# A selective scan laid out as 8 channels by 16 states on the partitions

## The chip, the cores and the metric

The kernel runs on one core of a Trainium2 chip. The time is device time in microseconds (us), from one launch; the figure compared is the median of runs. The engines are TensorE (PE), VectorE (DVE), ScalarE (ACT) and GpSimd (POOL); SyncE (SP) issues nearly all DMAs.

## What is computed

Two "metaformer" layers on x of 2 x 96 channels x 128 x 128 pixels, fp32. Layer 0's mixer is four selective scans (Mamba) over the 16,384 pixels in four orders: by rows, by rows backwards, by columns, by columns backwards. Cut to the part that matters (192 inner channels, 16 states, rank 6):

```python
xc, z = split(x @ in_w.T);  xc = silu(causal_conv4(xc) + conv_b)
dt_raw, B, C = split(xc @ xproj_w.T)             # 6, 16, 16
dt = softplus(dt_raw @ dt_w.T + dt_b);  A = -exp(A_log)
h_t[d, s] = exp(dt_t[d] * A[d, s]) * h_{t-1}[d, s] + dt_t[d] * u_t[d] * B_t[s]
y_t[d]    = sum_s h_t[d, s] * C_t[s]             # u is xc
out = ((y + Dp * xc) * silu(z)) @ outp_w.T       # four of these, then a fusing matmul
```

Before it stands a channel layernorm; after it a quantised FFN, a 3 x 3 convolution and a second FFN.

## The kernel before

For each of the 2 batches three stages run: `normalize`, `mamba`, `ffn_and_conv`. Only `mamba` is touched by the change.

`mamba` runs the four directions as two pairs (by rows with by columns; the two backward ones). A pair has 2 x 192 = 384 channels, three groups `g` of 128. A **step** is 512 tokens of one pair: 2 pairs x 32 = 64 steps a batch. Within a step there are 24 **units**; a unit is one group and two states. The tokens lie along the free dimension, 128 channels on the partitions. Group 1 holds 64 channels of each direction, interleaved by small DMAs (`mix`).

For a unit the work is:
- SP fetches, by DMA from DRAM, the rows of B and of C for four states, spread over the 128 partitions (`row_tile`, line 335; 1 MB each, one of each for two units).
- POOL makes dt x u x B for four states (`b_part`, line 339), and adds what the state entering the step brings to the first token (343).
- ACT makes `da` = exp(dt x A), two states, into PSUM (`decay`, 349); `da` has three buffers of two PSUM banks.
- DVE runs the recurrence over 512 tokens as one scan instruction for each state (`scan`, 353).
- DVE multiplies by C (line 441); for one unit in four (`BY_POOL`) POOL does it (360).
- ACT copies the last token's state to `hst` (442).
- PE adds the states up in PSUM, with an identity as weights (`sums`, 357), onto y, which starts as Dp x xc (448). At a group's end DVE multiplies y by silu(z) (`gated`, 364), and PE projects (372, 374).

The order of instructions on every engine is written out by hand. One loop over all units k issues, in this order: the fetch for unit k+6 and POOL's product for unit k+2 (both for even k), slot (k, 0), the first scan of unit k, what stands `behind` unit k-1 (its product with C, the `hst` copy, the sums), `decay` for unit k+2, the second scan of unit k, the fetch of C, slot (k, 1). The slots hold the next step's prologue (input DMAs, convolution and gate matmuls and their evictions by ACT, silu, the rows of dt, B and C, softplus, dt x u), placed by a list of unit numbers (lines 308 to 323). All prologue matmuls and the projection share one PSUM bank, `misc`. Each engine takes its instructions strictly in this order. Silu and softplus each load another activation table, and exp's table is loaded again after them (`preload_act_table_set`).

Of the kernel before, what the change touches and what calls it, by code (L numbers as in the profile page):

```python
# [23 lines left out]
T = 512  # L24
# [9 lines left out]
C_AHEAD = 2  # L34
AHEAD = 2
BY_POOL = tuple((g, s) for g in range(3) for s in (0, 8))
# [5 lines left out]
def tile_metaformer(ctx: ExitStack, tc: tile.TileContext, a: dict, out: bass.AP):  # L42
# [38 lines left out]
    amat = cpool.tile([128, 2, NG, S], F32, name="amat")  # L81
# [3 lines left out]
    def prep(st):  # L85
# [9 lines left out]
        alog, dskip = load("alog", (128, 2, NG, S)), load("dskip", (128, 2, NG))  # L95
# [89 lines left out]
    def mamba(acc, xnr, xnc):  # L185

        with ExitStack() as st:
            pool = lambda n, bufs, **kw: st.enter_context(tc.tile_pool(name=n, bufs=bufs, **kw))

            io, gen, one, mixp, two = (pool(*p) for p in (("io", 2), ("gen", 4), ("one", 1), ("mixp", 1), ("two", 2)))  # L190
# [3 lines left out]
            hst = one.tile([128, NG, S], F32, name="hst")  # L194
            enter = one.tile([128, NG, S], F32, name="enter")
# [5 lines left out]
            def inproj(pi, g, w, src, taps):  # L201

                ps = misc()
                for k in taps:
                    se = {"start": k == taps[0], "stop": k == taps[-1]}
                    for d, rows, lo, hi in (
                        ((0, slice(0, 128), 0, 128),),
                        ((0, slice(0, 64), 128, 192), (1, slice(64, 128), 0, 64)),
                        ((1, slice(0, 128), 64, 192),),
                    )[g]:  # L210
                        nc.tensor.matmul(ps[rows, :], w(PAIRS[pi][d], k, lo, hi), src[d][:, k : k + T], **se)  # L211
                return ps

            def prologue(pi, i, d):
# [5 lines left out]
                def load():  # L220
# [9 lines left out]
                    d["dtu"], d["yg"] = [], []  # L230

                def conv(g):
                    d["ps"] = inproj(pi, g, lambda dd, k, lo, hi: inx[:, dd, k, lo:hi], src, (0, 1, 2, 3))

                def conv_out(g):
                    if g == 1:
                        d["xc"] = two.tile([128, NG, T], F32, name="xc")
                    t = mixed("xc") if g == 1 else d["xc"][:, g, :]
                    nc.scalar.activation(t, d["ps"], AF.Identity, bias=convb[:, pi, g : g + 1])  # L239

                def gate(g):
                    d["ps"] = inproj(pi, g, lambda dd, k, lo, hi: inz[:, dd, lo:hi], src, (3,))

                def gate_out(g):
                    if g == 1:
                        d["sz"] = two.tile([128, NG, T], F32, name="sz")
                    nc.scalar.copy(mixed("sz") if g == 1 else d["sz"][:, g, :], d["ps"])  # L247

                def mixed(name):
                    d["mix", name] = mixp.tile([128, T], F32, name="mix")  # L250
                    return d["mix", name]

                def mix(name):

                    for k in range(2):
                        nc.sync.dma_start(d[name][k:128:2, 1, :], d["mix", name][64 * k : 64 * k + 64, :])
# [17 lines left out]
                def rows_to_dram():  # L274

                    d["bcd"] = rows_d.tile([2, S // 4, 2, 4, T], F32, name="bcd")
                    nc.sync.dma_start(d["bcd"].rearrange("k q d s t -> (k q d s) t"), d["rows"][BCO:, :])


# [11 lines left out]
                def softplus(lo, hi):  # L291
                    t = d["dt"][:, lo:hi, :]
                    nc.scalar.activation(t, t, AF.Softplus)
                    nc.scalar.preload_act_table_set("natural_log_exp_and_others")

                def dt_u(g):
                    dtu = gen.tile([128, T], F32, name="dtu")
                    nc.gpsimd.tensor_tensor(dtu, d["dt"][:, g, :], d["xc"][:, g, :], ALU.mult)  # L298
                    d["dtu"].append(dtu)

                def entry(g):

                    nc.scalar.activation(enter[:, g, :], amat[:, pi, g, :], AF.Exp, scale=d["dt"][:, g, 0:1])

                first = pi == 0 and i == 0
                at = [(-3, 1, load), (3, 0, partial(mix, "xc")), (11, 0, partial(silu, "xc"))]
                at += [(9, 0, partial(mix, "sz")), (31, 1, partial(silu, "sz"))]
                at += [(12, 0, rows), (13, 1, rows_out), (14, 0, rows_to_dram)]  # L310
                for g, k in ((1, 1), (0, 5), (2, 9)):
                    at += [(k, 0, partial(conv, g)), (k + 1, 1, partial(conv_out, g))]
                for g, k in ((1, 7), (0, 18), (2, 21)):
                    at += [(k, 0, partial(gate, g)), (k + 1, 0, partial(gate_out, g))]
                soft = ((0, 1, 16), (1, 3, 26)) if first else ((0, 3, 17),)
                for x0, x1, k in soft:
                    at += [(k, 1, partial(softplus, x0, x1))]
                for g, k in enumerate((14, 24, 25) if first else (14, 15, 16)):
                    at += [(k, 0, partial(dt_in, g)), (k + 1, 0, partial(dt_out, g))]
                for g, k in enumerate((19, 27, 29)):  # L320
                    at += [(k, 0, partial(dt_u, g))]
                    if i > 0:
                        at += [((20, 24, 29)[g], 1, partial(entry, g))]
# [5 lines left out]
            def row_tile(d, g, s, k, ahead):  # L329

                t = gen.tile([128, 4, T], F32, name=f"row{k}", bufs=ahead + 1)

                src = d["bcd"][k, s // 4] if g == 1 else d["bcd"][k, s // 4, g // 2 : g // 2 + 1]
                n = src.shape[0]
                nc.sync.dma_start(t, src[None].broadcast_to((128 // n, n, 4, T)))
                return t

            def b_part(i, d, g, s, b):
                nc.gpsimd.tensor_tensor(b, d["dtu"][g][:, None, :].broadcast_to((128, 4, T)), b, ALU.mult)  # L339
                if i > 0:  # L340
                    if s == 0:
                        nc.gpsimd.tensor_tensor(enter[:, g, :], enter[:, g, :], hst[:, g, :], ALU.mult)
                    nc.gpsimd.tensor_tensor(b[:, :, 0], b[:, :, 0], enter[:, g, s : s + 4], ALU.add)

            def decay(pi, d, g, s):

                da = ps_w.tile([128, 2, T], F32, name="da")
                for j in range(2):
                    nc.scalar.activation(da[:, j, :], d["dt"][:, g, :], AF.Exp, scale=amat[:, pi, g, s + j : s + j + 1])  # L349
                return da  # L350

            def scan(j, da, b, h):
                nc.vector.tensor_tensor_scan(h[:, j, :], da[:, j, :], b[:, j, :], 0.0, ALU.mult, ALU.add)  # L353

            def sums(s, y, c):
                for j in range(2):
                    nc.tensor.matmul(y, ident, c[:, j, :], start=False, stop=s + j == S - 1)  # L357

            def by_pool(h, c):
                nc.gpsimd.tensor_tensor(c, h, c, ALU.mult)  # L360

            def gated(pi, d, g, y):
                t = d["sz"][:, g, :]
                nc.vector.tensor_tensor(t, y, t, ALU.mult)  # L364
                d["yg"].append(t[:, ::-1] if pi == 1 else t)
# [18 lines left out]
            units = [(g, s) for g in range(NG) for s in range(0, S, 2)]  # L384
# [30 lines left out]
            def fetch(k, n, ahead, m):  # L415
                if k < total:
                    t = row_tile(state[k // nu], *units[k % nu], n, ahead)
                    m[k], m[k + 1] = t[:, 0:2, :], t[:, 2:4, :]
                    if n == 0:
                        quads[k] = t  # L420

            def feed(k):

                if k < total:
                    n = k // nu
                    b_part(steps[n][1], state[n], *units[k % nu], quads.pop(k))

            def feed_decay(k):
                if k < total:
                    n = k // nu  # L430
                    das[k] = decay(steps[n][0], state[n], *units[k % nu])
# [3 lines left out]
            def behind(k):  # L435

                n, u = divmod(k, nu)
                (pi, i), d, (g, s) = steps[n], state[n], units[u]
                h, c = hs.pop(k), cs.pop(k)
                if (g, s) not in BY_POOL:  # L440
                    nc.vector.tensor_tensor(c, h, c, ALU.mult)  # L441
                nc.scalar.copy(hst[:, g, s : s + 2], h[:, :, T - 1])  # L442
                if s == 0:
# [8 lines left out]
                if (g, s) in BY_POOL:  # L452
                    later(k + 1, 1, True, by_pool, h, c)
                    later(k + 3, 1, True, sums, s, y, c)
                else:
                    sums(s, y, c)
                if k == total - 1:
                    gated(pi, d, g, y)
                if s == S - 2 and g > 0:
                    later(k + 4, 0, True, project, pi, i, d, g)  # L460
                    later(k + 5, 1, False, collect, pi, d, g)

            for m, (n, ahead) in ((bs, (0, B_AHEAD)), (cs, (1, C_AHEAD))):
                for k in range(ahead):
                    fetch(2 * k, n, ahead, m)
# [3 lines left out]
            for k in range(total + 6):  # L469
                n, u = divmod(k, nu)  # L470
                if u == nu - 3:

                    prepare(n + 2)
                if k % 2 == 0:
                    fetch(k + 2 * B_AHEAD, 0, B_AHEAD, bs)
                    feed(k + AHEAD)
                issue(k, 0)
                if k < total:
                    (g, s) = units[u]
                    da, b = das.pop(k), bs.pop(k)  # L480
                    hs[k] = b if (g, s) in BY_POOL else da
                    scan(0, da, b, hs[k])
# [3 lines left out]
                if k < total:  # L486
                    scan(1, da, b, hs[k])
                if k % 2 == 0:
                    fetch(k + 2 * C_AHEAD, 1, C_AHEAD, cs)
# [110 lines left out]
def _layout(v):  # L600
# [4 lines left out]
    perm = np.arange(2 * DI)  # L605
# [63 lines left out]
```

## Time and profile before

| | us |
|---|---|
| median of 3 runs | 11,546.39 (11,545.31 to 11,548.33) |
| the profiled execution | 11,556.77 |
| its span, first to last instruction | 11,555.0 |
| PE busy | 10,435.0 |
| DVE busy | 10,421.6 |
| POOL busy | 9,672.3 |
| ACT busy | 7,901.7 |

Busy time is the union of an engine's instructions over the whole span. A matmul's record overlaps the next one's, so PE's busy share says less than the distance between starts. A group line gives line, engine, operation, output <- inputs, shapes and count; then busy us and the mean ns of one; then the engine's idle time just ahead of these instructions and what ended most of it. A time line gives start, duration, engine, line and tile names. An fp32 matmul appears as two records.

### The profile page before, as it was taken

How to read it: one execution, taken by the hardware profiler on the slowest of the kernel's cores; microseconds unless marked ns; L12 is line 12 of the kernel's file. 1: busy time of each engine (PE TensorE's matmuls, PEld its weight loads, DVE VectorE, ACT ScalarE, POOL GpSimd, SP SyncE). 2: the span in 40 equal slices, each digit the busy share in tenths (PEclk: the TensorE clock that was granted, in tenths of full speed). 3: DMA queues.
4: the chain of work that ended last, by engine and by line, in shares of the span. 5: the costliest groups of instructions: out<-in, count | busy, mean ns of one | idle time of the engine just before them, and what ended most of it. 6: DMA issues, size and time to landing. Idle time of an engine off the chain costs nothing. (4 is left out here: it accounts for less than half of the span.)

```text
span 11555.0 us, 94102 instructions
## 1 busy us (share of the span) xinstructions
PE 10435.0 (90%) x24208; PEld 3971.4 (34%) x24208; DVE 10421.6 (90%) x10127; ACT 7901.7 (68%) x13564; POOL 9672.3 (84%) x4700
## 2 busy tenths in 40 slices
PE   7999999999999999989989999999999999999899
PEld 2333333333333333333323333333333333333333
DVE  6999999999999999994469999999999999999944
ACT  6767767677677677665567677677676776776655
POOL 5999999999999999991159999999999999999911
PEclk8999999999999999999989999999999999999999
DMA  7888888888888888880068888888888888888800
GB/s 263 335 329 333 333 332 332 330 331 333 329 332 333 330 331 333 329 322 19 26 243 334 328 331 334 330 333 333 333 331 329 332 332 329 331 333 329 319 13 13
DMA packets 540755, 3416.96 MB, mean 296 GB/s; under 512 B 67532, under 2 KB 68652, under 8 KB 143832
## 3 DMA queue, kind: packets, MB, share of 16 engines
q1 hardware_dynamic: 539960, 3410.16, 76.8%
q8 instruction: 196, 3.21, 0.1%
q14 instruction: 343, 2.81, 0.1%
q0 software_dynamic: 256, 0.79, 0.0%
HBM read 3289.04 MB, written 54.53 MB: 289 GB/s over the span
## 5 line engine op out<-in xcount | busy, mean ns | idle before, releaser
L339 POOL TENSOR_TENSOR row<-dtu,row 128x2048 f32<-128x2048 f32 x1536 | 6948.9, 4524 | 283.3 <-DMA row<-bcd 281.6
L357 PE MATMUL y<-row,ident 128*128 128x512 f32 x12288 | 5690.6, 603 | 700.0 <-DVE row L441 699.9
L353 DVE TENSOR_TENSOR_SCAN da<-da,row 128x512 f32<-128x512 f32 x4608 | 5456.9, 1214 | 38.9 <-ACT da L349 5.2
L349 ACT ACTIVATE da<-dt,amat 128x512 f32<-128x512 f32 x6144 | 4246.9, 691 | 170.2
L357 PEld LDWEIGHTS y<-row,ident 128*128 128x128 f32 x12288 | 2256.8, 190 | 4008.4 <-issue 2243.5
L441 DVE TENSOR_TENSOR row<-da,row 128x1024 f32<-128x1024 f32 x2304 | 2776.7, 1205 | 70.2 <-DMA row<-bcd 70.0
L442 ACT COPY hst<-da 128x2 f32<-128x2 f32 x2304 | 368.9, 160 | 2652.2 <-DVE row L441 2649.3
L360 POOL TENSOR_TENSOR row<-row,row 128x1024 f32<-128x1024 f32 x768 | 1807.4, 2353 | 223.0 <-DVE row L353 147.5
L353 DVE TENSOR_TENSOR_SCAN row<-da,row 128x512 f32<-128x512 f32 x1536 | 1852.4, 1206 | 91.9 <-POOL row L339 84.1
L211 PE MATMUL misc<-xa,inx 96*64 96x512 f32 (+1 forms) x2048 | 946.1, 605 | 50.0 <-ACT mix L239 26.8
L211 PE MATMUL misc<-xb,inx 96*64 96x512 f32 (+1 forms) x2048 | 952.3, 608 | 33.6 <-ACT hst L442 24.2
L564 POOL TENSOR_TENSOR acc<-acc,y 96x512 f32<-96x512 f32 x128 | 147.4, 1151 | 991.5 <-DVE y L563 991.5
L298 POOL TENSOR_TENSOR dtu<-dt,xc 128x512 f32<-128x512 f32 x384 | 487.4, 1269 | 106.0 <-DMA xb<-xnc 99.8
L576 PE MATMUL pc<-pad,kw 96*96 96x512 f32 x1152 | 566.4, 593 | 0.0
L211 PEld LDWEIGHTS misc<-xa,inx 96*64 96x64 f32 (+1 forms) x2048 | 327.3, 165 | 581.2 <-issue 438.0
L448 PE MATMUL y<-xc,dmat 128*128 128x512 f32 x768 | 419.5, 628 | 103.6 <-DVE sz L364 103.6
L374 PE MATMUL misc<-sz,gmat 128*96 128x512 f32 x1024 | 484.1, 595 | 0.0
L284 PE MATMUL misc<-rows,dtw 12*128 12x512 f32 x768 | 434.3, 645 | 50.6 <-ACT dt L289 37.9
L364 DVE TENSOR_TENSOR sz<-y,sz 128x512 f32<-128x512 f32 x384 | 264.6, 689 | 229.5 <-PE y L357 198.0
L136 DVE TENSOR_TENSOR xq<-xm,rs 96x512 fp8e5<-96x512 f32 x128 | 87.9, 687 | 392.2 <-ACT rs L132 392.2
L211 PEld LDWEIGHTS misc<-xb,inx 96*64 96x64 f32 (+1 forms) x2048 | 316.5, 164 | 361.9 <-issue 214.1
L372 PE MATMUL misc<-acc,ident 96*96 96x512 f32 x512 | 387.6, 842 | 57.3 <-ACT sz L247 53.8
(76 smaller groups left out, 7449.9 us busy)
## 6 DMA issues: line engine op xcount, KB each, us to landing
row<-bcd SPq DMA_DIRECT2D x3072, 1024.0 KB, 7.4
xc<-mix SPq DMA_DIRECT2D x256, 128.0 KB, 5.4
sz<-mix SPq DMA_DIRECT2D x256, 128.0 KB, 8.9
xa<-xnr SPq DMA_DIRECT2D x124, 193.1 KB, 8.6
xb<-xnc SPq DMA_DIRECT2D x124, 193.1 KB, 8.7
bcd<-rows SPq DMA_DIRECT2D x128, 128.0 KB, 9.5
acc<-in_x_dram SPq DMA_DIRECT2D x16, 768.0 KB, 5.7
xnr<-xn SPq DMA_DIRECT2D x16, 768.0 KB, 4.3
```

The costliest lines, as they stand in the source:

```text
L211: nc.tensor.matmul(ps[rows, :], w(PAIRS[pi][d], k, lo, hi), src[d][:, k : k + T], **se)
L284: nc.tensor.matmul(d["ps"], w, d["rows"][0 : 2 * RK, :], start=True, stop=True)
L298: nc.gpsimd.tensor_tensor(dtu, d["dt"][:, g, :], d["xc"][:, g, :], ALU.mult)
L339: nc.gpsimd.tensor_tensor(b, d["dtu"][g][:, None, :].broadcast_to((128, 4, T)), b, ALU.mult)
L349: nc.scalar.activation(da[:, j, :], d["dt"][:, g, :], AF.Exp, scale=amat[:, pi, g, s + j : s + j + 1])
L353: nc.vector.tensor_tensor_scan(h[:, j, :], da[:, j, :], b[:, j, :], 0.0, ALU.mult, ALU.add)
L357: nc.tensor.matmul(y, ident, c[:, j, :], start=False, stop=s + j == S - 1)
L360: nc.gpsimd.tensor_tensor(c, h, c, ALU.mult)
L374: nc.tensor.matmul(d["po"], gmat[:, pi, 2 * g - 2 + k, :], d["yg"][g - 1 + k], start=False, stop=k == 1)
L441: nc.vector.tensor_tensor(c, h, c, ALU.mult)
L448: nc.tensor.matmul(y, dmat[:, pi, g, :], d["xc"][:, g, :], start=True, stop=False)
L576: nc.tensor.matmul(pc, kw[:, t, :], rows, start=t == 0, stop=t == 8)
```

## The change

The partitions of a scan now hold 16 states x 8 channels, states outermost (p = 8 s + c), in place of 128 channels of one state.

- B and C depend on the state and the token alone, so one spread tile for a step and both directions (`bc`, 1 MB) replaces the fetched rows. It is written to DRAM and read back once a step (`rows_to_dram`, `spread`).
- dt x u depends on the channel, so it has to be spread over the 16 states: it is written to DRAM by four DMAs for each group, and `quad_tile` reads 4 x 8 channels back, spread over the states, 1 MB for two units. POOL multiplies it by B in place (`b_part`).
- dt is spread by PE: two matmuls a unit with a 0/1 matrix `sel`, each over 32 rows of the array, into the `da` banks; ACT takes exp in place.
- The entering state: two ACT products on the first token of `da`, and a scan that starts from 1, replace POOL's additions.
- The sum over states is a matmul with a 0/1 matrix `fold` whose output is 32 partitions wide: four for two units, onto four column tiles of y.
- Group 1 is no longer interleaved, so `mix` and its DMAs go. The convolutions are issued in two halves, and the prologue's slots move. POOL takes seven products of 24 in place of six. `c` has its own four buffers; pooled products are written in place.

```diff
-BY_POOL = tuple((g, s) for g in range(3) for s in (0, 8))
+C_BUFS = 4
+NQ = 4
+BY_POOL = ((0, 1), (0, 4), (1, 1), (1, 2), (1, 4), (2, 1), (2, 4))
...
+                def spread():
+                    d["bc"] = two.tile([128, 2, 2, T], F32, name="bc")
+                    nc.sync.dma_start(d["bc"], d["bcd"][:, None].broadcast_to((S, 8, 2, 2, T)))
...
-                def entry(g):
-                    nc.scalar.activation(enter[:, g, :], amat[:, pi, g, :], AF.Exp, scale=d["dt"][:, g, 0:1])
+                def dtu_to_dram(g):
+                    t = rows_d.tile([NQ, 8, 4, T], F32, name=f"dtud{g}")
+                    rows = t.rearrange("q d c t -> (q d) c t")
+                    for c in range(4):
+                        nc.sync.dma_start(rows[:, c, :], d["dtu"][32 * c : 32 * c + 32, :])
+                    d["dtud"][g] = t
...
+                at = [(-6, 1, load), (5, 0, partial(silu, "xc")), (30, 1, partial(silu, "sz"))]
+                at += [(6, 0, rows), (7, 1, rows_out), (8, 0, rows_to_dram), (11, 0, spread)]
+                for g, k in ((1, -3), (0, -1), (2, 1)):
+                    at += [(k, 0, partial(conv, g, (0, 1))), (k, 1, partial(conv, g, (2, 3))), (k + 1, 1, partial(conv_out, g))]
+                for g, k in ((1, 12), (0, 14), (2, 16)):
+                    at += [(k, 0, partial(gate, g)), (k + 1, 0, partial(gate_out, g))]
+                for g in range(NG):
+                    at += [(8 + g, 0, partial(dt_in, g)), (9 + g, 0, partial(dt_out, g))]
+                at += [(11, 1, softplus)]
+                for g, k in enumerate((13, 24, 26) if first else (13, 15, 17)):
+                    at += [(k, 0, partial(dt_u, g)), (k + 1, 0, partial(dtu_to_dram, g))]
...
-            def row_tile(d, g, s, k, ahead):
-                t = gen.tile([128, 4, T], F32, name=f"row{k}", bufs=ahead + 1)
-                src = d["bcd"][k, s // 4] if g == 1 else d["bcd"][k, s // 4, g // 2 : g // 2 + 1]
-                n = src.shape[0]
-                nc.sync.dma_start(t, src[None].broadcast_to((128 // n, n, 4, T)))
+            def quad_tile(d, g, q):
+                t = gen.tile([128, 4, T], F32, name="quad", bufs=B_AHEAD + 1)
+                nc.sync.dma_start(t, d["dtud"][g][q][None].broadcast_to((S, 8, 4, T)))
                 return t
...
-                nc.gpsimd.tensor_tensor(b, d["dtu"][g][:, None, :].broadcast_to((128, 4, T)), b, ALU.mult)
-                if i > 0:
-                    if s == 0:
-                        nc.gpsimd.tensor_tensor(enter[:, g, :], enter[:, g, :], hst[:, g, :], ALU.mult)
-                    nc.gpsimd.tensor_tensor(b[:, :, 0], b[:, :, 0], enter[:, g, s : s + 4], ALU.add)
+                nc.gpsimd.tensor_tensor(b, row.broadcast_to((128, n, 4 // n, T)), b, ALU.mult)
...
                 da = ps_w.tile([128, 2, T], F32, name="da")
                 for j in range(2):
-                    nc.scalar.activation(da[:, j, :], d["dt"][:, g, :], AF.Exp, scale=amat[:, pi, g, s + j : s + j + 1])
+                    rows = slice(64 * u + 32 * j, 64 * u + 32 * j + 32)
+                    nc.tensor.matmul(da[:, j, :], sel[rows, q, :], d["dt"][rows, g, :], start=True, stop=True)
+                for j in range(2):
+                    c = 2 * u + j
+                    nc.scalar.activation(da[:, j, :], da[:, j, :], AF.Exp, scale=amat[:, pi, g, q, c : c + 1])
+                if i > 0:
+                    for j in range(2):
+                        c = 2 * u + j
+                        nc.scalar.activation(da[:, j, 0:1], da[:, j, 0:1], AF.Copy, scale=hst[:, g, q, c : c + 1])
                 return da
...
-            def scan(j, da, b, h):
-                nc.vector.tensor_tensor_scan(h[:, j, :], da[:, j, :], b[:, j, :], 0.0, ALU.mult, ALU.add)
-            def sums(s, y, c):
-                for j in range(2):
-                    nc.tensor.matmul(y, ident, c[:, j, :], start=False, stop=s + j == S - 1)
+            def scan(i, j, da, b, h):
+                nc.vector.tensor_tensor_scan(h[:, j, :], da[:, j, :], b[:, j, :], float(i > 0), ALU.mult, ALU.add)
+            def sums(q, y, cs):
+                for u, c in cs:
+                    for j in range(2):
+                        rows = slice(64 * u + 32 * j, 64 * u + 32 * j + 32)
+                        nc.tensor.matmul(y[rows, :], fold[:, q, :], c[:, j, :], start=False, stop=q == NQ - 1)
...
+                    c = gen.tile([128, 2, T], F32, name="c", bufs=C_BUFS)
+                    nc.vector.tensor_tensor(c, h, c_rows(d, g, u), ALU.mult)
...
+                if u == 1:
+                    pair = [k - 1 + j for j in range(2) if (g, 2 * q + j) in BY_POOL]
+                    args = q, y, [(j, cs.pop(k - 1 + j)) for j in range(2)]
+                    if pair:
+                        later(pair[-1] + 3, 1, True, sums, *args)
+                    else:
+                        sums(*args)
```

The weights' layouts on the host follow (no group is permuted any more; `alog` by partition, `sel` and `fold` new). The DMA scratch in the program's set-up is made smaller (`dynamic_dma_scratch_size=4096`).

## The prediction

> **What bounds the kernel now.** I read the page's totals first, then one step of the selective scan by its window, then its time lines engine by engine. A step is 512 tokens of two directions, 24 units of two states; 2 batches x 64 steps = 128 steps. One step, from one gating product to the same one a step later, by engine (PE, PE weights, DVE, ACT, POOL; busy us and count):
>
> ```profile
> 3017.77:3096.72 78.95, 72.01 (x166) 27.24 (x166) 76.53 (x69) 55.71 (x97) 74.35 (x37) 1.00 0.86 333
> ```
>
> 128 x 78.95 = 10,106 us of the 11,555.0 us span; normalisation, FFN and convolution are the other 1,449 us, and the change leaves them alone. DVE works 97% of the step and POOL 94%; ACT only 71%. What they do, from the costliest groups:
>
> ```profile
> L339 POOL TENSOR_TENSOR row<-dtu,row 128x2048 f32<-128x2048 f32 x1536 | 6948.9, 4524 | 283.3 <-DMA row<-bcd 281.6
> L357 PE MATMUL y<-row,ident 128*128 128x512 f32 x12288 | 5690.6, 603 | 700.0 <-DVE row L441 699.9
> L353 DVE TENSOR_TENSOR_SCAN da<-da,row 128x512 f32<-128x512 f32 x4608 | 5456.9, 1214 | 38.9 <-ACT da L349 5.2
> L349 ACT ACTIVATE da<-dt,amat 128x512 f32<-128x512 f32 x6144 | 4246.9, 691 | 170.2
> L441 DVE TENSOR_TENSOR row<-da,row 128x1024 f32<-128x1024 f32 x2304 | 2776.7, 1205 | 70.2 <-DMA row<-bcd 70.0
> L442 ACT COPY hst<-da 128x2 f32<-128x2 f32 x2304 | 368.9, 160 | 2652.2 <-DVE row L441 2649.3
> ```
>
> The scans wait 5.2 us for ACT in the whole run. ACT's idle time lies ahead of the little copy L442: it waits for DVE's product L441, and the exponentials (L349) of the unit two ahead follow at once. In the time line of ACT (start, duration):
>
> ```profile
> 3042.85 0.67 ACT L289 ACTIVATE dt<-misc,dtb 128x512 f32<-128x512 f32 x1
> 3043.42 0.18 ACT L442 COPY hst<-row 128x2 f32<-128x2 f32 x1
> 3043.50 1.42 ACT L349 ACTIVATE da<-dt,amat 128x512 f32<-128x512 f32 x2
> 3044.93 1.28 ACT L293 ACT_TABLE_LOAD   x1
> 3046.23 1.48 ACT L293 ACTIVATE dt<-dt 128x1536 f32<-128x1536 f32 x1
> 3047.73 1.28 ACT L294 ACT_TABLE_LOAD   x1
> 3049.02 0.16 ACT L442 COPY hst<-da 128x2 f32<-128x2 f32 x1
> ```
>
> A table change with its function holds ACT for 4.1 us, three times a step. It costs DVE next to nothing now, because exp needs only dt, which lies ready: PE is on no path into the scan.
>
> PE, in the same step:
>
> ```profile
> 3036.85 1.12 PE L284 MATMUL misc<-rows,dtw 12*128 12x512 f32 x2 [0.26 <-ACT dt L289]
> 3070.45 0.59 PE L211 MATMUL misc<-xa,inx 96*64 96x512 f32 x1
> 3070.46 0.59 PE L211 MATMUL misc<-xb,inx 96*64 96x512 f32 x1
> 3070.88 0.59 PE L211 MATMUL misc<-xa,inx 96*64 96x512 f32 x1
> 3070.89 0.59 PE L211 MATMUL misc<-xb,inx 96*64 96x512 f32 x1
> ```
>
> An fp32 matmul is two records 0.43 us apart: 0.86 us of PE, 1.12 us from start to result when alone. Two 64-column tiles start 0.01 us apart and the next pair 0.43 us later: column tiles run side by side.
>
> **What the edits save.** DVE: seven of 24 products on POOL in place of six. 48 scans + 17 products at 1.12 us from start to start (2.33 us for two, 3.58 for three) + three gatings at 0.61 = 74.6 us; now 75.7. POOL: 12 x 4.55 + 7 x 2.32 + 3 x 1.24 = 74.5 us; the twelve 0.20 us entry additions go. So DVE and POOL alone would give about 74.6 us a step. DMA: 24 tiles of 1 MB become 12, plus 1 MB for B and C, 0.75 MB of dt x u written, and the reads of x: some 14 MB against 26 (333 GB/s x 78.95). That ends POOL's 283 us and DVE's 70 us of waits for rows, in those 74.6. Mixing DMAs go from SP; it gains 12 writes of dt x u (64 KB) and two waits (dt x u landed before the quad is read, four units later, 13 us; bcd landed before it is spread, three units). bcd now lands in 9.5 us, so I price both at nothing; uncovered, each would hold SP's fetches for the rest of that time, less the three quads fetched ahead. PE's sums are 12 groups of four 32-column tiles, by the pair above side by side: 12 x 0.86 in place of 48 x 0.86, 31 us less. The new spreading matmuls (line 336 of the new kernel; L329 and up below mean its lines where they are not in the fences) are 24 pairs on two row tiles. PE falls to about 60 us. The layout of the weights, the two constants and the smaller DMA scratch stand outside the loop: nothing.
>
> **What the edits add, on the path.** The da of unit k+2 is now made by PE, then ACT in place, then two one-element ACT products with the entering state, then the scan. There are three da buffers. In the order of instructions of the new program, L336 for most units waits for the hst copy of the unit whose buffer it takes, and ACT runs that copy only after the exponentials of the unit before. So each unit goes round ACT (exp k+1) -> ACT (hst) -> PE (L336) -> ACT (exp k+2), and everything ahead of L336 in PE's queue, which itself waits for an ACT eviction, joins the round. A bare round: exp pair 1.42, two small products 0.40, hst 0.2, then ACT idle while L336 runs, 1.12 + hand-overs 0.08 = 1.2; in all 3.2 us, where DVE needs 3.36 us for a unit with its product and 2.24 without. With a prologue step in it: the eviction of group 1's conv stands behind exp of unit 24 (slot 22,1), the first half of group 0's conv (slot 23,0; 1.75 us) needs the one misc buffer that this frees, and L336 of unit 25 stands behind that half. I followed the three queues through one step in this way; ACT sets the pace nearly throughout.
>
> ACT's own work: 24 exp pairs x 1.42 = 34.1; 48 one-element products x 0.20 = 9.6; 24 hst copies x 0.19 (3001.80 to the next start at 3001.99) = 4.6; three table blocks x 4.1 = 12.3; evictions of conv, gate, dt, rows and output 7.0 (0.57 to 1.05 each, less 0.08 where the next starts early). Sum 67.6; now 56.
>
> The one-element products are not in this trace. Nearest below are the 0.08 us by which a following start trails; above, L303 (16 elements, a scale per partition) with 0.295. I take 0.20, near L442's 0.160 plus a wait for exp's result. Ends: -5.8 and +4.6 us a step. Exp reading PSUM: between L247's PSUM copy, 0.58, and 0.69; I keep 0.71 with the wait. End: -5.3.
>
> ACT's waits for PE, link by link (L336 with hand-over 1.2):
> - with a prologue matmul ahead that waited for ACT: second conv half-pair 1.75 + y start 0.86 + 1.15, less 0.2 hst = 3.6; output projection (three matmuls) 3.55; dt of group 0 with sums 2.7; dt of group 1 with y start 2.7; dt of group 2 1.85; the other two convs 2.75 each. Sum 19.9.
> - bare L336: five times 1.2 = 6.0. L336 with sums or DVE's product ending late: 1.65 + 1.7.
> - behind other PE work or a scan: conv remainder 0.55, gating and y start 1.4, buffer of a pooled unit (freed by its second scan) 2.15, sums of two pairs 2.3. Sum 6.4.
> Together 35.7; in the remaining six links L336 is done before ACT gets there.
>
> 67.6 + 35.7 = 103.3 us a step, 24.35 over now; DVE then idles 29 us of it. 128 x 24.35 = 3,117; on the profiled execution's 11,556.8 us that is 14,674, and the median of runs lies 10 us under it: **14,660 us**.
>
> Whether row tiles run side by side no row here shows. Nearest is the column pair (0.01 us apart): taken. Other end: one after the other, +0.86 in 18 links, +15.5 us. Going from 128-wide tiles to 64-wide and back costs 0.09 us each way (L357 x4 from 3009.42, next start 3011.23 in place of 3011.14); two more switches a unit, half on the round: +2 at most. POOL's C product for a pooled unit now waits for the hst copy, and the next quad's product is queued behind it: 0 to +2.
>
> [...]
>
> **Rivals.**
> - *DVE stays the bound (faster).* If L336 and ACT ran far enough ahead, the step is 74.6: 11,557 - 128 x 4.35 = 11,000. For it: PE and ACT each have fewer us of work than DVE. It decides once ACT's waits for PE fall under 74.6 - 67.6 = 7 us of the 35.7; equal to now at 11. Three buffers and one ACT queue speak against it. 6%.
> - *Row tiles run one after the other.* 103.3 + 15.5 = 118.8: 16,660. 14%.
> - *Cheap ACT, same round.* Both ACT ends: 92.2 us, 13,250. 15%.
> - *Round shorter than I have it*, half the PE waits hidden: 85.5, 12,390. 9%.
> - The round as worked, 97 to 112 us: 56%.
>
> **Numbers.** Forecast 14,660. Leaving out the faster case, most of the half-hidden one and the top of the serial one gives 12,700 to 16,500. About 0.2% is what a measurement can tell from no change: faster 0.06, within 0.01, slower 0.93.
>
> **What would show it.** Right: DVE busy near 72% of a step, scans waiting for ACT L343, ACT waiting for PE L336, L336 pairs 0.01 us apart, POOL idle, DMA near 40%. A spread of 0.43 or more between the two row tiles means the serial rival. Wrong: scans back to back at 1.12, ACT idle ahead of hst as now.

## Result and the profile after

The changed kernel takes 19,062.43 us (median of 4 runs, 19,039.46 to 19,113.52) against 11,546.12 (11,545.31 to 11,548.33): **1.6515 times as long, 95% interval 1.6479 to 1.6552**. The forecast was 14,660 with a range of 12,700 to 16,500. The direction held; the size did not.

The page's totals of the changed kernel, with the row of the granted clock:

```profile
span 19042.8 us, 121991 instructions
PE 14568.6 (77%) x36496; PEld 3717.3 (20%) x36496; DVE 10527.2 (55%) x9999; ACT 8680.4 (46%) x19138; POOL 9621.1 (51%) x2968
PEclk7666666666666666667966666666666666666679
```

DVE, which worked 97% of a step, is down to 55%. No engine is full. PE shows 77% although, by the prediction's count, it has less to do than before: the granted clock fell from 0.989 to 0.668 over the span, to six or seven tenths all through the scan. One step by its window (PE, PE weights, DVE, ACT, POOL busy, then clock, DMA share, GB/s):

```profile
5040.24:5180.13 139.89, 107.80 (x264) 25.66 (x264) 77.52 (x68) 62.26 (x141) 73.92 (x22) 0.62 0.46 107
```

DVE and POOL have as much work a step as before (77.5 and 73.9 us); the step is now 140 us long around it. The groups that answer to those of before:

```profile
L339 ACT ACTIVATE da<-da,amat 128x512 f32<-128x512 f32 x6144 | 4071.0, 663 | 9102.0 <-PE da L336 8504.0
L347 DVE TENSOR_TENSOR_SCAN da<-da,quad 128x512 f32<-128x512 f32 x4352 | 5284.3, 1223 | 5151.8 <-ACT da L343 3530.0
L329 POOL TENSOR_TENSOR quad<-bc,quad 128x2048 f32<-128x2048 f32 x1536 | 6921.8, 4513 | 1892.6 <-DMA quad<-dtud 1785.0
L336 PE MATMUL da<-dt,sel 32*128 32x512 f32 x12288 | 4930.5, 906 | 1580.0 <-ACT hst L444 1447.9
```

Read them from the right. The scans, which waited 5.2 us for ACT in the whole run, wait 3,530. The exponentials waited 9,102 us, 71 us a step, nearly all for the spreading matmuls; and these wait for ACT's hst copy. That is the round that was forecast. POOL waits 1,785 us for quads, for which nothing was priced. The chain that ended last:

```profile
PE 51%; ACT 23%; DMA 9%; DVE 7%; POOL 4%; issue 3%; another core or an unknown queue 2%; SPq 1%; ACTq 0%; POOLq 0%; DVEq 0%
PE da L336 15%; PE misc L215 13%; ACT da L339 10%; PE y L353 6%; DMA dtud<-dtu 6%; POOL quad L329 4%; PE misc L259 3%; DVE da L347 3%; PE misc L279 3%; PE pc L579 3%; PE y L450 2%; ACT da L343 2%; DMA quad<-dtud 2%; PE misc L374 2%
```

**The round at half clock.** PE's time line in the same step (start, duration, then in brackets the idle time before it and what ended it):

```profile
5116.79 3.78 PE L215 MATMUL misc<-xa,inx 96*128 96x512 f32 x4 [2.54 <-ACT hst L444]
5120.50 2.08 PE L336 MATMUL da<-dt,sel 32*128 32x512 f32 x4
5122.50 3.78 PE L215 MATMUL misc<-xa,inx 96*128 96x512 f32 x4
...
5128.33 1.13 PE L336 MATMUL da<-dt,sel 32*128 32x512 f32 x4
5131.99 2.22 PE L215 MATMUL misc<-xb,inx 96*128 96x512 f32 x4 [2.54 <-ACT hst L444]
5134.00 1.92 PE L450 MATMUL y<-xc,dmat 128*128 128x512 f32 x2
5135.85 2.07 PE L336 MATMUL da<-dt,sel 32*128 32x512 f32 x4
```

The same spreading pair (two fp32 matmuls, four records) takes 1.13 us or 2.08. At 1.13, the time of one lone fp32 matmul of two records, both row tiles are within one matmul's time: they do run side by side. Half a convolution, priced at 1.75 us, takes 3.78. PE is fast at 5128, waits 2.54 us for ACT's exponentials, products and eviction, and at 5134 it is slow again. The windows show the granted clock with it (the third figure from the end), 1.00 up to there and 0.50 behind it:

```profile
5126.80:5133.60 6.80, 4.26 (x24) 1.40 (x17) 3.99 (x5) 2.36 (x6) 0.00 (x0) 1.00 0.66 154
5133.70:5150.60 16.90, 14.42 (x21) 4.01 (x19) 7.17 (x7) 4.18 (x11) 6.82 (x2) 0.50 0.26 62
```

In ACT's time line the round through 5116 to 5129 shows as its two waits:

```profile
5122.68 1.36 ACT L339 ACTIVATE da<-da,amat 128x512 f32<-128x512 f32 x2 [5.90 <-PE da L336]
5129.56 1.36 ACT L339 ACTIVATE da<-da,amat 128x512 f32<-128x512 f32 x2 [5.01 <-PE da L336]
```

**The hole of the quads.** The chain of waits, a little earlier in that step:

```profile
5072.99 1.15 DVE da L347
5074.19 0.51 SPq L322
5074.76 0.58 SPq L299
...
5076.31 12.01 DMA dtud<-dtu
5088.39 0.08 issue
5088.48 0.10 POOL dtu L292
5088.58 1.12 issue
5089.70 4.51 POOL quad L329
```

SP's next quad fetch (L322) waits for its buffer, here until a scan is done; over the whole run its waits are put down to the sums of y (8,954 us; behind a pooled unit they come late) and to scans (5,787 us). The writes of dt x u (L299) are queued behind it on SP, then need 12 us to land; POOL's next dt x u (L292) and quad product (L329) stand behind that landing. From 5074.19 to the end of the product at 5094.21 it is 20 us.

**The step added up.** All of ACT's waits ahead of L339 in the step sum to 72.8 us: 15.0 in the six waits from 5073.47 to 5100.61, where the quads hold everyone, and 57.8 in the rest. ACT works 62.3, and 4.8 us are other small gaps: 62.3 + 57.8 + 15.0 + 4.8 = 139.9. The forecast had 67.6 + 35.7 = 103.3. And 35.7 / 0.62, the clock granted in this step, is 57.6. So my reading was that the links had been counted rightly, their clock and the quads wrongly. It is a reading of one step: the six waits hold links that the 35.7 counts too, and nothing in the trace says how long they would have been without the quads. The experiments test it.

### The profile page after: what moved, and what is told of

Same layout as the page of the kernel before. It is cut to its first block, busy times and chain, and to the rows that moved or that the text cites. A ratio compares the mean times of both kernels' runs of the same rounds, so it can differ in the third digit from the quotient of the medians.

```text
span 19042.8 us, 121991 instructions
## 1 busy us (share of the span) xinstructions
PE 14568.6 (77%) x36496; PEld 3717.3 (20%) x36496; DVE 10527.2 (55%) x9999; ACT 8680.4 (46%) x19138; POOL 9621.1 (51%) x2968
## 4 chain that ended last, share of the span: by engine, by line
PE 51%; ACT 23%; DMA 9%; DVE 7%; POOL 4%; issue 3%; another core or an unknown queue 2%; SPq 1%; ACTq 0%; POOLq 0%; DVEq 0%
PE da L336 15%; PE misc L215 13%; ACT da L339 10%; PE y L353 6%; DMA dtud<-dtu 6%; POOL quad L329 4%; PE misc L259 3%; DVE da L347 3%; PE misc L279 3%; PE pc L579 3%; PE y L450 2%; ACT da L343 2%; DMA quad<-dtud 2%; PE misc L374 2%
## 5 line engine op out<-in xcount | busy, mean ns | idle before, releaser
L339 ACT ACTIVATE da<-da,amat 128x512 f32<-128x512 f32 x6144 | 4071.0, 663 | 9102.0 <-PE da L336 8504.0
L347 DVE TENSOR_TENSOR_SCAN da<-da,quad 128x512 f32<-128x512 f32 x4352 | 5284.3, 1223 | 5151.8 <-ACT da L343 3530.0
L329 POOL TENSOR_TENSOR quad<-bc,quad 128x2048 f32<-128x2048 f32 x1536 | 6921.8, 4513 | 1892.6 <-DMA quad<-dtud 1785.0
L336 PE MATMUL da<-dt,sel 32*128 32x512 f32 x12288 | 4930.5, 906 | 1580.0 <-ACT hst L444 1447.9
L360 POOL TENSOR_TENSOR quad<-quad,bc 128x1024 f32<-128x1024 f32 x896 | 2104.5, 2349 | 6117.4 <-ACT hst L444 6113.6
L347 DVE TENSOR_TENSOR_SCAN quad<-da,quad 128x512 f32<-128x512 f32 x1792 | 2164.4, 1214 | 2049.6 <-ACT da L343 1507.4
L353 PE MATMUL y<-c,fold 128*32 128x512 f32 x8704 | 2749.9, 901 | 109.5 <-DVE c L443 108.9
L443 DVE TENSOR_TENSOR c<-da,bc 128x1024 f32<-128x1024 f32 x2176 | 2619.3, 1204 | 0.2
L336 PEld LDWEIGHTS da<-dt,sel 32*128 32x128 f32 x12288 | 1287.5, 253 | 5128.9 <-issue 2182.9
L353 PE MATMUL y<-quad,fold 128*32 128x512 f32 x3584 | 1553.4, 962 | 5.7 <-POOL quad L360 5.7
L343 ACT ACTIVATE da<-da,hst 128x1 f32<-128x1 f32 x5952 | 1149.9, 232 | 96.1
```

The source lines that it names most:

```text
L329: nc.gpsimd.tensor_tensor(b, row.broadcast_to((128, n, 4 // n, T)), b, ALU.mult)
L336: nc.tensor.matmul(da[:, j, :], sel[rows, q, :], d["dt"][rows, g, :], start=True, stop=True)
L339: nc.scalar.activation(da[:, j, :], da[:, j, :], AF.Exp, scale=amat[:, pi, g, q, c : c + 1])
L343: nc.scalar.activation(da[:, j, 0:1], da[:, j, 0:1], AF.Copy, scale=hst[:, g, q, c : c + 1])
L353: nc.tensor.matmul(y[rows, :], fold[:, q, :], c[:, j, :], start=False, stop=q == NQ - 1)
L360: nc.gpsimd.tensor_tensor(h, h, c_rows(d, g, u), ALU.mult)
```

## Experiments

Ratios are to the kernel before in the same comparison; the changed kernel stands at 1.6515. Saved us a step are differences of medians over 128.

**1. The clock: matmuls with weights of zero.** After each unit's L336 pair, into the sum that is open, except at a group's end:

```diff
                 feed_decay(k + AHEAD)
+                if 0 < k < total and k % 8 != 0:
+                    for _ in range(2):        # warm; range(1) in warm1
+                        nc.tensor.matmul(ys[k - 1], nought, state[n]["bc"][:, 1, 0, :], start=False, stop=False)
```

> Adds work and changes nothing else: after each unit's two spreading matmuls, two fp32 matmuls with all-zero weights are added onto the open y (nought x bc), 42 a step, 0.86 us of PE each at full clock. Theory 1 (the granted PE clock of 0.67 is what made the round ACT-PE-ACT 138 us instead of 103): the clock rises to 0.85 or more, the L336 pair goes from 2.08 us back to 1.13 us, and the step falls to 110-120 us, 15,500-16,800 us in all. Rival (PE's work or the quads' DMA path sets the step, the low clock is only its companion): the added 36 to 72 us of PE work per step lengthen it, 19,500-23,000 us.

> One zero-weight matmul after each unit's spreading pair in place of two (21 a step, 0.86 us each at full clock), which fits under ACT's 2 us for the unit. Theory 1 (the low clock lengthens every PE link of the round): granted clock 0.85 or more, and without the cost of the second filler the step goes to 115-128 us, 16,200-17,900 us. Rival (the clock matters little): no less than the 18,340 us of two fillers.

Measured: warm 18,339.54 us, 1.5887 (1.5841 to 1.5933), clock 0.908; warm1 18,313.43, 1.5860 (1.5814 to 1.5906), clock 0.838. The clock rose by far; the time fell 4%. The theory of the clock had 16,800 us at most for warm and 17,900 for warm1, so it missed both; the rival had 19,500 or more for warm and missed too. In warm1 the group of L336 (a line lower by two there) and ACT's wait for it:

```profile
L341 ACT ACTIVATE da<-da,amat 128x512 f32<-128x512 f32 x6144 | 4068.5, 662 | 8134.3 <-PE da L338 7552.7
L338 PE MATMUL da<-dt,sel 32*128 32x512 f32 x12288 | 4410.9, 763 | 930.6 <-ACT hst L446 918.7
```

One record went from 906 to 763 ns, but the fillers stand in the same queue (10% of warm1's chain), and the quads' hole stays (DMA 9% of the chain, as without fillers). The clock alone, bought at this price, takes back little of the loss.

**2. hst on DVE, and the quads' data and buffers.**

```diff
-                nc.scalar.copy(hst[:, g, q, 2 * u : 2 * u + 2], h[:, :, T - 1])
+                nc.vector.tensor_copy(hst[:, g, q, 2 * u : 2 * u + 2], h[:, :, T - 1])      # hst_dve
-                    d["dtud"][g] = t         # static: the writes to t stay, but every step's quads
+                    d["dtud"][g] = once[g]   # are read from one copy of the first step's dt x u
-                t = gen.tile([128, 4, T], F32, name="quad", bufs=B_AHEAD + 1)
+                t = gen.tile([128, 4, T], F32, name="quad", bufs=B_AHEAD + 2)               # q5
```

> The copy of the last token's state to hst is done by DVE instead of ACT, so L336 no longer waits for a copy that stands behind the exponentials of the unit before. Theory 1b (the round goes through ACT's copy): L336 of a unit runs while ACT still does the unit before; bare links lose the wait for PE, 8 to 12 us of 138 at the low clock; with the prologue steps' rounds left, 17,000-18,000 us. Rival (the round is closed by the prologue evictions and by PE's own work, the copy is beside it): within 1%, 18,900-19,200 us.

> The quads of all steps are read from a DRAM copy of the first step's dt x u of the same pair of directions' first step (so the result is not the reference's); every write of dt x u to DRAM stays. So no quad waits for a write of its own step. Theory 2 (the way of dt x u through DRAM holds SP and POOL, 14 us a step of POOL waiting for quads): 8 to 14 us a step less, 17,300-18,000 us. Rival (hidden behind the round): within 1%.

> Five quad buffers in place of four, the fetch still three pairs ahead. Theory 2b (SP's fetch waits for a quad that pooled sums still hold, and the dt x u writes queue behind that fetch): SP's wait for PE y goes, quads land in time, 8 to 14 us a step less, 17,300-18,000 us. Rival (the DRAM way or the round itself): within 1%.

Measured: hst_dve 18,593.74, 1.6107 (1.6060 to 1.6154); static 19,106.51, 1.6551 (1.6408 to 1.6695), no change, as its rival had it; q5 18,506.79, 1.6032 (1.5985 to 1.6078). hst_dve and q5 fall between their theories (18,000 or less) and their rivals (within 1%). In hst_dve L336's wait for the hst copy goes from 1,448 us to 253, but ACT's wait for L336 does not fall (8,796 us, from 8,504) and POOL's wait for quads rises from 1,785 us to 3,028: the wait taken away comes back elsewhere.

In static a quad reads old data and the time is the same. So a quad does not wait for its own step's dt x u to land. It waits for a buffer: with a fifth, POOL's wait for quads is gone,

```profile
L329 POOL TENSOR_TENSOR quad<-bc,quad 128x2048 f32<-128x2048 f32 x1536 | 6915.5, 4515 | 24.4 <-DMA quad<-dtud 24.2
```

and DMA falls from 9% of the chain to 0, yet only 4.3 us a step are saved of a 20 us hole: PE grows from 51% to 63% of the chain. ACT still waits 8,343 us for L336 there, 65 a step: the wait behind was nearly as late.

**3. The prologue half a unit later.** Those of its matmuls that wait for an eviction, and the output projection, are issued behind the unit's L336 instead of ahead of it, so that ACT's eviction and the next L336 no longer have them in between; the second half of a convolution follows at the start of the next unit:

```diff
-                at += [(6, 0, rows), (7, 1, rows_out), (8, 0, rows_to_dram), (11, 0, spread)]
+                at += [(6, 1, rows), (7, 1, rows_out), (8, 0, rows_to_dram), (11, 0, spread)]
-                    at += [(k, 0, partial(conv, g, (0, 1))), (k, 1, partial(conv, g, (2, 3))), (k + 1, 1, partial(conv_out, g))]
+                    at += [(k, 1, partial(conv, g, (0, 1))), (k + 1, 0, partial(conv, g, (2, 3))), (k + 1, 1, partial(conv_out, g))]
-                    at += [(k, 0, partial(gate, g)), (k + 1, 0, partial(gate_out, g))]
+                    at += [(k, 1, partial(gate, g)), (k + 1, 0, partial(gate_out, g))]
-                    at += [(8 + g, 0, partial(dt_in, g)), (9 + g, 0, partial(dt_out, g))]
+                    at += [(8 + g, 1, partial(dt_in, g)), (9 + g, 0, partial(dt_out, g))]
-                    later(k + 4, 0, True, project, pi, i, d, g)
+                    later(k + 4, 1, True, project, pi, i, d, g)
```

> Only the prologue's places change: every prologue matmul that waits for an ACT eviction (convolution halves, gates, rows, dt) and the projection is issued half a unit later, behind the L336 pair of its unit in PE's queue in place of ahead of it. Theory 3 (the prologue's eviction and the matmul that waits for it close the round between two exponentials, as the prediction's list says, 20 of 36 us): at a low clock 25 to 35 us a step less, 14,600-15,900 us. Rival (PE is simply full at the low clock, wherever the work stands; 108 of 140 us busy): less than 5%, 18,100 us or more.

Measured: 16,138.82, 1.3977 (1.3936 to 1.4017): 22.8 us a step, the largest of any single edit, if less than the 25 to 35 expected. ACT's wait for L336 falls by 30%:

```profile
L339 ACT ACTIVATE da<-da,amat 128x512 f32<-128x512 f32 x6144 | 4075.5, 663 | 6062.7 <-PE da L336 5962.9
```

Nothing was taken from PE's work here, only its place. The granted clock rose from 0.668 to 0.751 with no filler, so the gain holds a share of the clock, which no run separates from the shorter queue.

**4. The repairs together.** three is slots, hst_dve and q5; four also moves the gates' silu from slot 30 to 19.

> The later slots, hst copied by DVE, and five quad buffers together. If the three act on three different waits (prologue rounds, ACT's copy, quads), the gains add or more: the step 90 to 105 us, 12,900-14,900 us, PE busier and the granted clock above 0.8. Rival (one wait is behind all three and takes over from the one removed): no better than the later slots alone by 2%.

> As 'three', and silu of the gates, a 4.1 us block on ACT, stands at unit 19 of the step before in place of unit 6 (one unit after the other silu). If ACT's blocks are what is left, 3 to 5 us a step less than 'three'; else the same within 1%.

Measured: three 14,452.62, 1.2517 (1.2480 to 1.2553); four 14,313.94, 1.2396 (1.2360 to 1.2432). Singly the three edits save 22.8 + 3.7 + 4.3 = 30.8 us a step, together 36.0: they stand in line, as three's theory had it. four is within 1% of three, so ACT's blocks were not what was left. ACT still waits 36 us a step for L336 in four.

**5. The scan's output out of PSUM.** To free L336 of the product and the hst copy, the scans of DVE's units write the SBUF tile c, and the product is made in place there, on top of four:

```diff
-                    hs[k] = b if (units[u][0], u % 8) in BY_POOL else da
+                    hs[k] = b if (units[u][0], u % 8) in BY_POOL else gen.tile([128, 2, T], F32, name="c", bufs=C_BUFS)
...
+                c = h      # hst is copied first, then the product in place
```

> The kernel with all four repairs (labelled four) and one more: the scans of units that DVE multiplies write the SBUF tile c instead of da in PSUM, the last column is copied to hst before the product, and the product is made in place in c. So the spreading matmuls of unit k+2 wait only for the second scan of unit k-1, not for its product and its hst copy. Theory of the round (each unit goes DVE product, hst, PE, ACT, and PE's wait is exposed): the 36 us a step that ACT still waits for PE shrinks to under 10, DVE's 77 us a step becomes the bound, 10,700 to 11,800 us. Theory of the clock (PE at 0.78 of its clock needs some 83 us a step whatever it waits for): PE becomes the bound, 12,200 to 12,800 us, and the clock stays under 0.85. If neither the round nor the clock holds the steps, 14,200 to 14,400.

> The kernel labelled five with one matmul with weights of zero added to the open sum after each unit's spreading pair (21 us a step of PE at full clock). If five is held by a low clock: the clock rises to over 0.9 and the time falls by 2 to 6%. If five is held by DVE: no change within 1%. If PE's own work is the bound at full clock: slower by 5 to 15%.

Both expectations missed in all their cases: five 18,043.73, 1.5628 (1.5604 to 1.5651), 26% more than four; five_warm 18,378.82, 1.5909 (1.5882 to 1.5935). The time lines of five, DVE and then POOL, say why:

```profile
5019.41 0.34 DVE L443 COPY hst<-c 128x2 f32<-128x2 f32 x1
5019.79 5.52 DVE L445 TENSOR_TENSOR c<-c,bc 128x1024 f32<-128x1024 f32 x1
```

```profile
5019.69 4.53 POOL L329 TENSOR_TENSOR quad<-bc,quad 128x2048 f32<-128x2048 f32 x1
5024.18 2.24 POOL L292 TENSOR_TENSOR dtu<-dt,xc 128x512 f32<-128x512 f32 x1
```

DVE's product starts 0.10 us after POOL's and takes 5.52 us; it ends 1.1 us after POOL's, one product's time, as if it had stood still until POOL was done. The mean product went from 1,204 ns in four to 2,404; with da in PSUM none took over 1,225 there, though POOL was busy for 9,619 us. The little copies of hst, now from SBUF too, took 1,271 ns on the mean (148 in four, from PSUM). DVE's busy time grows by both from 10,842 us in four to 15,723, 38 us a step, and the step by 29. So the scan in place in PSUM, which holds L336 up, is what kept DVE's products in four free of POOL. The run says nothing on the round.

**6. Fillers on the repaired kernels.** One filler a unit on q5 and on four, and one in every second unit on four.

> The changed kernel with both single edits tried before, one filler matmul a unit (alone -3.9%, clock 0.84) and five quad buffers (alone -2.9%). If the two losses stand in line, each hidden behind the other when only one is taken away: 15,300 to 16,800 us (the hole of some 24 us a step that the quads leave in the run with fillers goes). If they only add: 17,500 to 17,900. If both took away the same waits: 18,200 to 18,400.

> The kernel labelled four (clock 0.78, ACT waits 36 us a step for the spreading matmuls) with one filler matmul a unit. Theory of the clock: clock 0.9, the spreading pair falls from some 1.6 to 1.2 us and the time to 13,400 to 13,900. Theory of the round alone: the fillers stand in PE's queue and the time stays within 2% or gets worse, 14,200 to 14,800.

> The kernel labelled four (14,314 us at a clock of 0.78) with a filler matmul in every second unit only; with one in every unit it took 14,038 at 0.96, the fillers being 11% of the chain of waits themselves. If the clock is worth what the fillers take back: clock 0.86 to 0.95 and 13,500 to 13,900. If the clock is worth little: 14,100 to 14,300.

Measured: warm1_q5 17,070.14, 1.4785 (1.4763 to 1.4807), clock 0.86; four_warm 14,037.56, 1.2158 (1.2138 to 1.2178), clock 0.959; four_half 14,294.76, 1.2385 (1.2366 to 1.2403), clock 0.875. Alone the fifth buffer saves 4.3 us a step and the filler 5.9; together 15.6. So each of the two losses hid in part behind the other; the time lies between the ranges for losses in line (16,800 at most) and for losses that add (17,500 at least). The sum of the step can be held against it: 62.3 + 35.7 / 0.86 + 4.8 = 108.6, and fillers are 11% of this run's chain, 14.7 us a step: 123.3. The step of the run, (17,070 - 1,449) / 128, is 122.0. But the same sum fails on q5, which has neither fillers nor the hole: 62.3 + 35.7 / 0.688 + 4.8 = 119.0, and its step is 133.3. So the forecast's links at the mean clock are not the whole of ACT's waits; what the other 14 us are stays open. In four the clock's rise about pays for the fillers and no more (four_warm -1.9%, between its two theories; four_half nothing). The share of the clock without fillers was not isolated by any run; for it stand the two durations of the same matmul, and a sum that fits one run and misses another.

**7. dt by DMA instead of row-tiled matmuls.** One part undone: dt goes to DRAM like dt x u and is read back spread, so exp reads SBUF and PE is out of the path; dt's own tile becomes single to make room. dt_dma_slots adds slots, hst_dve and the silu's move.

```diff
-                    nc.tensor.matmul(da[:, j, :], sel[rows, q, :], d["dt"][rows, g, :], start=True, stop=True)
-                    nc.scalar.activation(da[:, j, :], da[:, j, :], AF.Exp, scale=amat[:, pi, g, q, c : c + 1])
+                nc.sync.dma_start(t, d["dtd"][g][q][:, 2 * u : 2 * u + 2][None].broadcast_to((S, 8, 2, T)))   # five units ahead
+                    nc.scalar.activation(da[:, j, :], dq[:, j, :], AF.Exp, scale=amat[:, pi, g, q, c : c + 1])
```

> One part undone alone: dt is not spread by row-tiled matmuls but, like dt x u, written to DRAM and read back spread over the 16 states (512 KB a unit, four buffers, five units ahead), so that the exponentials read SBUF and PE is on no path into the scan; dt's tile is single instead of double to make room. Everything else is the changed kernel, the quads with their four buffers and the prologue's places too. Theory that PE's place between ACT and ACT (the round and its prologue matmuls) is the main loss: most of the 71 us a step that ACT waits for PE go, a step takes 85 to 105 us, 12,400 to 14,900 us; the granted clock stays as low as 0.67 or falls, since PE does less, and that no longer matters much. Theory that the detour of dt x u and SP's queue are the main loss: SP gets 24 more fetches and 12 more writes a step and the time stays or rises, 18,500 to 20,500.

> dt_dma with the prologue's matmuls half a unit later, the hst copies on DVE and the gates' silu moved (all of the kernel labelled four but its fifth quad buffer, for which there is no room). If dt_dma has taken PE off the path, these edits have little left to take: within 4% of dt_dma. If the prologue's places still matter through y and misc: 4 to 12% below it. Best case, DVE's 77 us a step: 11,400.

Measured: dt_dma 16,488.53, 1.4282 (1.4260 to 1.4305); dt_dma_slots 16,479.47, 1.4288 (1.4259 to 1.4316). The time falls 20.1 us a step with PE out of the path and the clock still 0.687, but less than expected (14,900 us at most), for a new bound: the window and the chain by engine and line of dt_dma

```profile
5000.00:6000.00 1000.00, 562.72 (x1408) 142.57 (x1408) 660.48 (x583) 545.76 (x1206) 634.80 (x191) 0.66 1.00 243
```

```profile
DMA 63%; ACT 13%; PE 10%; POOL 7%; issue 3%; DVE 2%; SPq 2%; POOLq 0%; ACTq 0%; DVEq 0%
DMA dq<-dtd 38%; DMA quad<-dtud 23%; ACT da L351 5%; POOL quad L337 4%; PE pc L600 3%; POOL quad L372 2%; PE misc L279 2%; PE xm L125 1%; PE v L131 1%; ACT L253 1%; ACT L252 1%; ACT xc L252 1%; ACT da L355 1%; DMA dtud<-dtu 1%; PE y L365 1%
```

The DMA engines are busy all the time, at 243 GB/s. The repairs of slots bring nothing on top (without dt_dma slots alone is a fall of 15.3%). That fits repairs which act only through PE's place ahead of exp, but does not show it: with the DMA engines full, a saving elsewhere could not come through either. Why 243 GB/s fills the engines here, where 333 took 86% of them before, was not tried.

No version came near the kernel before; the best, four_warm, is at 1.2158, 19 us a step over it. PE has 61% of its chain, fillers included, and ACT still waits 36 us a step for the spreading matmuls (4,572 us), so PE's path most likely still holds it; no run takes that apart.

## Why the prediction was wrong, step by step

**Right.** The sign, and the mechanism that set it: da made by PE between two steps of ACT, with the hst copy and the prologue's evictions in the round. slots moves only the prologue's place and takes back 22.8 us a step; dt_dma takes PE out of the path and takes back 20.1 before the DMA engines are full. The hst copy, moved alone, gave 3.7. Row tiles and column tiles run side by side (1.13 us a pair; eight records of the sums, four tiles, in 1.00 us), so the serial rival is out, though its 16,660 lies nearer to the result than the forecast does. Scans wait for L343, exp for L336, POOL idles: as listed. The rivals of a DVE bound and of a half-hidden round needed less waiting than the forecast, that of a cheap ACT no more than it, and there was more.

**ACT's own work**, 67.6 us: 62.3 measured. The exponential pair takes 1.36 for 1.42, the two one-element products 0.39 for 0.40. Small, and to the other side.

**ACT's waits for PE, 35.7 us: the term that failed first.** The run has 8,504 us of them, 66 a step. The term was summed with durations from a trace at clock 1.00, and nothing in the sum allows for a lower one. The round itself made PE wait for ACT in unit after unit: in the step shown PE has, among others, seven waits of 2.48 to 2.54 us, one of 3.54 and one of 6.21, and a granted clock of 0.62; links priced at 1.12 and 1.75 us took 2.08 and 3.78. In the step shown the waits outside the stretch of the quads are 57.8 us, 22.1 more than forecast. How much of this excess is the clock alone stays open: 35.7 / 0.62 gives it nearly all, but the same sum falls 14 us short in q5. That the waits brought the clock down fits the runs that put matmuls into them (0.668 without, 0.838 with one a unit, 0.908 with two). How long a wait it takes was not shown: the slow matmuls at 5134, at a granted clock of 0.50, follow one of 2.54 us. The gaps to count were those of every round.

**The two new waits on SP, priced at nothing: the term that failed second.** The cover named was three quads fetched ahead. The fetch waits for something else, its buffer, which a scan still reads (as in the hole shown) or which a pooled unit's C product and sums hold, and the writes of dt x u wait behind it in SP's queue. ACT's waits in that stretch of the step shown are 15.0 us, an upper end for its cost there; removed alone it gave 4.3 us, with the fillers 9.7 more than these alone. "Uncovered, each would hold SP's fetches" was said, and not followed to whoever holds the buffer.

Together -5.3 + 22.1 + 15.0 + 4.8 = 36.6 us over the forecast's 103.3 in the step shown; the mean over the run is 34.3, (19,062 - 1,449) / 128 less 103.3. **The range** failed with them: its upper end came from serial row tiles, and no case had PE's links slower all together, as they were here in the stretches at a granted clock of 0.50 (2.08 us for 1.13).

**DVE 72%, DMA 40%.** DVE has 55%, since the step is longer. DMA has 0.46 in a step of 140 us at 107 GB/s, where the old rate (0.86 at 333 GB/s) would have given 0.28: a byte cost about 1.7 times the engine time it did.

**Switches of the tiling**, +2 us at most by the row: the pair at 5128.33, at clock 1.00, takes 1.13 us from start to end. The last eight records of the sums in column tiles ahead of it start at 5127.36, 0.97 us earlier, where two records in a row are 0.86: 0.11 us for the switch, near the row's 0.09.

## What to carry to other kernels

When a change puts an engine into a round with another (ACT, PE, ACT), its durations from a trace in which it ran ahead may no longer hold, as here: price the whole round a second time with that engine's links as slow as a trace with such gaps has shown them (here 2.08 us for 1.13), and let the range reach there. For a prefetch, follow the queue to whoever holds the buffer that the next fetch needs, not only to the data. And before a PSUM operand is moved to SBUF to break a wait, see what POOL is doing at that moment (here 5.52 us for a product of 1.20).

## What the runs showed of the hardware

- PE's granted clock stayed at 0.6 to 0.7 through whole scans with PE "busy" 77%; in the windows above it was 1.00 or 0.50; matmuls with weights of zero in its gaps raised the mean from 0.67 to 0.84 (one a unit) and 0.91 (two), the prologue issued half a unit later, alone, to 0.75.
- A DVE product with both inputs in SBUF took 5.52 us beside a POOL product of 4.53 us that had started 0.10 us earlier (mean of all 2,404 ns; 1,204 with one input in PSUM).
- Reads that spread DRAM rows over 16 states filled the DMA engines at 243 GB/s; the old kernel's 1 MB tiles moved 333 GB/s at a DMA share of 0.86.
- Two row-tiled fp32 matmuls took 1.13 us at clock 1.00, as one alone (1.12); at 0.50 they took 2.08.
